# Row and column sums of the features: two of the three additions as accumulating transfers

## The chip, the cores and the metric

One core of one Trainium2 chip runs one program that computes the whole result. The metric is the device time of the program in microseconds, the median over its runs. The time before is 2430.3 us (two runs, 2430.04 and 2430.55). Engine names are those of the profile: PE is TensorE, PEld its weight loads, DVE is VectorE, ACT is ScalarE, POOL is GpSimd, SP is SyncE, whose queue issues most transfers.

## The reference

Eight sequences x of 512 tokens by 256 features go through a mixture of eight experts and a shared expert (all in float32, every expert on every token), and the gated result is added to x:

```python
g = jnp.einsum('bsd,edf->ebsf', h, Wg)
u = jnp.einsum('bsd,edf->ebsf', h, Wu)
expert_outs = jnp.einsum('ebsf,efd->ebsd', jax.nn.silu(g) * u, Wd)
expert_output = jnp.einsum('be,ebsd->bsd', gating_probs, expert_outs)
shared = jnp.einsum('bsf,fd->bsd', jax.nn.silu(h @ Sg) * (h @ Su), Sd)
sg = shared_gate_prob[:, :, None]
return (1.0 - sg) * expert_output + sg * shared      # and x is added
```

Here D = 256 and F = 1024. The gate of an expert for a sequence is one number, so the kernel multiplies the feature silu(g)*u by it ("coef") before the down product, and all experts of a sequence add up in one accumulator.

## The kernel before, in words

**Units.** The sequences are taken in two halves of four. For each half, each of the nine experts (the shared one is the ninth) and each of two groups of 512 columns of F there is a *unit*: 2 x 9 x 2 = 36 units, some 67 us each. In a unit four weight tiles i = 0..3 (128 columns of F each) meet four sequences j = 0..3, so there are sixteen features h(i, j) of 128 x 512.

**Fewer products.** The sixteen features are not made by sixteen plain products. The four diagonal ones are made in the *hub* of a unit (lines 503 to 540), and the others in *pairs*: for each (i, j) of PAIRS = (1,0), (0,2), (3,0), (1,2), (3,1), (3,2), three products give both h(j, i) and h(i, j) (R1_step and R_step, lines 549 to 571). For that, POOL makes *forms* of the weights: `at` (line 409), `u`, the difference of two `at` (w_difference, line 427), and `wb` (w_sums, line 433). The unit's `at` of tile 3 and its first `u` and `wb` are made on POOL at the start of the unit (lines 822 to 831); `at` of tiles 1 and 2 one unit ahead. The forms of the activations (`v`, `b`) are made once in the first unit, stored, and loaded again for each later unit through SP's queue, a pair or more ahead.

**Finish.** ACT takes silu of the gate product from its bank (line 490), and DVE multiplies it by the up product and by coef into a feature tile h (line 495).

**Down products.** These, too, use fewer products: for each pair two products with the pair's features and one with their difference X (line 581), and for each index n one product with the *row sum* n, the sum of h(n, l) over l, and one with the *column sum* n, the sum of h(k, n) over k. So each unit needs eight sums of four features each, three additions apiece: 24 additions of 128 x 512 on POOL (add_sum, line 589). The last unit makes its down products directly and needs no sums, so 35 units have them, 840 additions in all. The down products of a unit run from the middle of its pairs into the hub of the next unit (function `down`, line 605): first pairs 0 to 4, then row sum 0 and column sum 0, pair 5, then column sum 1, row sum 1, column sum 2, row sum 2, column sum 3 and row sum 3. Lines 634 and 657 are their matmuls.

**Order of work.** The queues of PE and POOL are written out by hand (`manual_schedule`, line 945): the main loop (lines 974 to 1011) walks a string of G (one product of gate and up) and D (one step of down), and the POOL instructions come between them. The additions are queued by h_sums after each pair (line 585 to 587), and the loop takes one from the queue at every second G of the later part of a unit (line 989) and at each of the first G of the next (line 991). Whatever is still queued when a sum is read is issued just ahead (flush_sums). The order on DVE, ACT and SP is set by the scheduler.

**Tiles.** Before, each feature has a tile of its own out of 11 (hpool), and each sum a tile out of 8 (sumpool). Six tiles of zpool hold the differences f of the hub and the rows that `prepare` loads for the second half.

Of the kernel before, what the change touches and what calls it, by code (L numbers as in the profile page):

```python
# [10 lines left out]
F32 = mybir.dt.float32  # L11
AF = mybir.ActivationFunctionType
ALU = mybir.AluOpType
# [4 lines left out]
def kernel(  # L18
# [38 lines left out]
    B, S, D = x.shape  # L57
    E, _, F = Wg.shape
    P = 128
# [15 lines left out]
    xpool = ctx.enter_context(tc.tile_pool(name="xp", bufs=4))  # L75
# [1 line left out]
    bpool = ctx.enter_context(tc.tile_pool(name="b", bufs=2))  # L77
    ppool = ctx.enter_context(tc.tile_pool(name="p", bufs=6))
    ddpool = ctx.enter_context(tc.tile_pool(name="dd", bufs=8))
    hpool = ctx.enter_context(tc.tile_pool(name="h", bufs=11))  # L80
    sumpool = ctx.enter_context(tc.tile_pool(name="sum", bufs=8))
    tpool = ctx.enter_context(tc.tile_pool(name="t", bufs=2))
    apool = ctx.enter_context(tc.tile_pool(name="ap", bufs=1))
    zpool = ctx.enter_context(tc.tile_pool(name="z", bufs=6))
    spool = ctx.enter_context(tc.tile_pool(name="s", bufs=4))
    dpool = ctx.enter_context(tc.tile_pool(name="d", bufs=2))
    iopool = ctx.enter_context(tc.tile_pool(name="io", bufs=2))
# [4 lines left out]
    ps_o = ctx.enter_context(tc.tile_pool(name="ps_o", bufs=1, space=PSUM))  # L92

    ident = const.tile([P, P], F32, name="ident")
    make_identity(nc, ident)

    gp = nc.gpsimd
# [25 lines left out]
    def issue_after(later, *first):  # L123

        for at in first:
            tc.add_manual_dep(
                later.ins,
                at.ins.name,
                mybir.DependencyInfo(
                    mybir.DependencyClass.NoSync, mybir.DependencyReason.DATA  # L130
                ),
                reason="issue order",
            )
# [25 lines left out]
    def load_rows(pool, tag, b):  # L159
        rows = []  # L160
        for c in range(2):
            if pool is not xpool:
                t = pool.tile([P, 2, D], F32, tag=tag, name=f"xin{b}_{c}")
            elif c == 0:
                both = pool.tile([P, NT, D], F32, tag=tag, name=f"xin{b}")
            if pool is xpool:
                t = both[:, 2 * c : 2 * c + 2]
            nc.sync.dma_start(
                t, x[b].rearrange("(p t) d -> p t d", t=NT)[:, 2 * c : 2 * c + 2, :]
            )  # L170
            rows.append(t)
        return rows
# [134 lines left out]
    def first_order(u, made, *what):  # L307

        if u.n == 0:
            u.issued[what] = made  # L310
            for late, early in BEHIND.items():
                if what in (late, early) and late in u.issued and early in u.issued:
                    issue_after(u.issued[late], u.issued[early])
# [67 lines left out]
    for h in range(NH):  # L381
        for e in range(NE):
            for g in range(GRP):
                u = Unit()
                u.n, u.h, u.e, u.g = len(units), h, e, g
                u.opens = e == 0 and g == 0
                u.closes = e == NE - 1 and g == GRP - 1
                u.name = f"{h}_{e}_{g}"
                u.raw, u.at, u.U, u.W, u.V, u.VB = {}, {}, {}, {}, {}, {}
                u.Ps, u.Ds, u.f, u.bank, u.h_ = {}, {}, {}, {}, {}  # L390
                u.sg, u.rows, u.cols, u.X, u.store = {}, {}, {}, {}, []
                u.sums, u.puts, u.unscaled = [], (), []
                u.ad, u.Ud, u.Wd = {}, {}, {}
                u.issued = {}
                units.append(u)

    def load_w(u, i, queue=nc.sync):
        if i not in u.raw:
            u.raw[i] = wpool.tile([P, 2, 2, P], F32, tag="w", name=f"w{u.name}_{i}")
        t = u.raw[i]  # L400
        for m in range(2):
            queue.dma_start(
                t[:, m],
                weights(u.e)[m][:, ts(NI * u.g + i, P)].rearrange(
                    "(k p) f -> p k f", p=P
                ),
            )
# [79 lines left out]
    def finish(u, m, i, j, bank):  # L487
        if m == 0:
            s = spool.tile([P, S], F32, tag="sg", name=f"sg{i}{j}_{u.name}")
            nc.scalar.activation(s, bank, AF.Silu)  # L490
            u.sg[i, j] = s
        else:
            b = NI * u.h + j
            t = hpool.tile([P, S], F32, tag="h", name=f"h{i}{j}_{u.name}")
            made = ve.scalar_tensor_tensor(  # L495
                t, u.sg[i, j], coef[:, u.e, b : b + 1], bank, ALU.mult, ALU.mult
            )
            latest_h[:] = u, made
            first_order(u, made, *(("h", i) if i == j else ("h", i, j)))
            u.h_[i, j] = t  # L500
# [27 lines left out]
    def Q_step(u, i, m):  # L528
        bank = u.bank[i, i, m]
        nc.tensor.matmul(  # L530
            bank, u.at[i][:, m], xhub[u.h, i][:, 1],
            start=False, stop=True, skip_group_check=True,
        )
        t = ddpool.tile([P, S], F32, tag="dd", name=f"D{i}{m}_{u.name}")
        u.Ds[i, m] = t
        if u.n == 0 and m == 1:
            nc.scalar.copy(t, bank)
        finish(u, m, i, i, bank)
        if u.n or m == 0:
            nc.scalar.copy(t, bank)  # L540
# [33 lines left out]
    def h_sums(u, p):  # L574


        i, j = PAIRS[p]
        if u.n + 1 == len(units):
            return
        u.X[p] = tpool.tile([P, S], F32, tag="t", name=f"X{p}_{u.name}")  # L580
        made = (gp if closes(u) and p in (1, 2, 3, 4) else ve).tensor_tensor(  # L581
            u.X[p], u.h_[j, i], u.h_[i, j], ALU.subtract
        )
        first_order(u, made, "X", p)
        for k, l in ((i, j), (j, i)):
            for which, n in (("rows", k), ("cols", l)):
                u.sums.append((which, n, (k, l)))

    def add_sum(u):
        which, n, at = u.sums.pop(0)  # L590
        sums = getattr(u, which)
        first = n not in sums
        if first:
            sums[n] = sumpool.tile([P, S], F32, tag="sum", name=f"{which}{n}_{u.name}")
        gp.tensor_tensor(sums[n], u.h_[n, n] if first else sums[n], u.h_[at], ALU.add)  # L595

    def flush_sums(u, which, n):
        while any(w == which and k == n for w, k, _ in u.sums):
            add_sum(u)

    def closes(u):

        return u.n + (2 if u.h + 1 == NH else 1) == len(units) * (u.h + 1) // NH
# [148 lines left out]
    def end_step(kind, i):  # L752

        b = NI * (NH - 1) + i
        if kind == "turn":
            t = iopool.tile([P, 2, S], F32, tag="io", name=f"end{i}")
            for r in range(2):
                ve.transpose(t[:, r], ends.pop((NH - 1, i, r)))
            ended[i] = t
        elif kind == "store":  # L760
            to = end_rows[i] = dram.tile([S, D], F32, tag=f"end{i}", name=f"endrows{i}")
            at = to.rearrange("(c r t) d -> r t c d", r=32, t=NT)
            for r in range(2):
                for q in range(4):
                    outgoing.append((
                        at[:, :, :, ts(4 * r + q, 32)],
                        ended[i][ts(q, 32), r].rearrange("r (t c d) -> r t c d", t=NT, d=32),
                    ))
        elif kind == "x":
            last_rows[i] = load_rows(xpool, "x", b)  # L770
        elif kind == "load":
            at = end_rows[i].rearrange("(p t) d -> p t d", t=NT)
            end_rows[i] = []
            for c in range(2):
                t = sumpool.tile([P, 2, D], F32, tag="sum", name=f"endin{i}_{c}")
                nc.sync.dma_start(t, at[:, 2 * c : 2 * c + 2])
                end_rows[i].append(t)
        else:
            for xr, t in zip(last_rows[i], end_rows[i]):
                gp.tensor_tensor(xr, xr, t, ALU.add)  # L780
# [31 lines left out]
    def gate_up(u, nxt):  # L812
# [12 lines left out]
        if u.n == 1:  # L825
            for _ in range(2):
                add_sum(units[0])
# [101 lines left out]
    for i in range(NI):  # L929
        c = CI[i]  # L930
# [21 lines left out]
    touch_banks()  # L952
    loaded = []
    for i in range(NI):
        loaded.append(load_rows(hpool, "h", i))
        if i:
            load_w(units[0], i)
    turning = turn_x(0, loaded)
# [8 lines left out]
    for u in units:  # L967
# [6 lines left out]
        for what in FIRST if u.n == 0 else LAST if nxt is None else OPENING if u.opens else ORDER:  # L974
            if what == "G":
# [8 lines left out]
                if nxt is None:  # L984
                    for what_, i in END_STEPS.get(nG, ()):
                        end_step(what_, i)
                if outgoing:
                    nc.sync.dma_start(*outgoing.pop(0))
                if nG > TAKE and nG % 2 == 0 and u.sums:
                    add_sum(u)  # L990
# [67 lines left out]
```

## Time and profile before

| what | value |
|---|---|
| median of the runs | 2430.3 us |
| profiled execution, first to last instruction (span) | 2427.7 us |
| PE busy | 2423.2 us (100%) |
| POOL busy | 2082.6 us (86%) |
| DVE busy | 1919.5 us (79%) |
| ACT busy | 1239.0 us (51%) |
| clock granted to PE, in every slice | 0.9 or more of full speed (mean 1.000) |
| DMA queue of SP: moved, share of 16 engines' span | 256.17 MB, 35.4% |
| POOL additions for the sums (line 595), four groups | 840, 1102.1 us |

The span is the profiled execution's own time as the profile shows it; the runs' times are taken from outside and lie 2.6 us above it. A row of the groups reads: line, engine, operation, output<-inputs by the program's names, shapes, xcount | busy us, mean ns of one | idle time of the engine just ahead of them, and what ended it. A row of a timeline reads: start in us, duration in us, engine, line and operation, and in brackets the idle time before it and who ended it. A row of waits reads: who waited <- for whom: us in total, times, the longest. In the rows of windows each engine's busy time stands with its count, then the granted clock, the DMA share and GB/s.

### The profile page before, as it was taken

To read this page: it belongs to the slowest core of one execution; us is meant where nothing else is said; L and a number is where in the kernel's file an instruction comes from. 1 tells how busy PE (TensorE), PEld (TensorE's weight loads), DVE (VectorE), ACT (ScalarE), POOL (GpSimd) and SP (SyncE) were. 2 spreads that over 40 slices of the span, in tenths; PEclk is the share of its full clock that TensorE was granted. 3 is DMA by queue.
4 is the path that set the end of the run, shared out by engine and by line. 5 is a ranking of instruction groups with operands and counts; after the bars stand their busy time and mean duration, and the time that the engine had idled before them with its cause. 6 is when DMAs were issued, how large, how long until landed. Compare 5 with 4: busy or idle time off the path is not lost.

```text
span 2427.7 us, 22771 instructions
## 1 busy us (share of the span) xinstructions
PE 2423.2 (100%) x5735; PEld 1085.3 (45%) x5735; DVE 1919.5 (79%) x2861; ACT 1239.0 (51%) x2294; POOL 2082.6 (86%) x2321
## 2 busy tenths in 40 slices
PE   9999999999999999999999999999999999999999
PEld 4444444444444444444444444444444444444446
DVE  8788888777777877787987777777877777777795
ACT  5555555554555454555455555555455555555542
POOL 7988888898988989898888888888888888888882
PEclk9999999999999999999999999999999999999999
DMA  4333333334333332334453322322333333323245
GB/s 161 108 111 107 110 98 100 117 117 126 104 122 104 103 113 94 108 112 124 119 124 110 91 84 91 92 87 90 100 104 104 95 97 90 92 87 96 79 132 145
DMA packets 221201, 257.92 MB, mean 106 GB/s; under 512 B 64016, under 2 KB 156432, under 8 KB 221072
## 3 DMA queue, kind: packets, MB, share of 16 engines
q1 hardware_dynamic: 220240, 256.17, 35.4%
q8 instruction: 48, 0.79, 0.1%
q14 instruction: 81, 0.66, 0.1%
q10 hardware_dynamic: 832, 0.30, 0.0%
HBM read 238.59 MB, written 17.83 MB: 106 GB/s over the span
## 4 chain that ended last, share of the span: by engine, by line
PE 100%; DVE 0%; issue 0%
PE c L565 31%; PE c L552 15%; PE c L530 10%; PE c L506 10%; PE r L657 7%; PE r L692 7%; PE b L634 5%; PE S L634 5%; PE q L657 5%; PE s L657 2%; PE tail L792 1%; PE B L634 0%; PE ptx L234 0%; PE touchg L372 0%; PE c L212 0%; PE ptx L208 0%
## 5 line engine op out<-in xcount | busy, mean ns | idle before, releaser
L565 PE MATMUL c<-b,wb 128*128 128x512 f32 x1728 | 847.1, 592 | 0.0
L490 ACT ACTIVATE sg<-c 128x512 f32<-128x512 f32 x576 | 343.7, 597 | 571.1 <-DVE c L570 330.3
L495 DVE SCALAR_TENSOR_TENSOR h<-sg,coef,c 128x512 f32<-128x512 f32 x576 | 427.5, 742 | 240.7 <-PE c L565 133.9
L565 PEld LDWEIGHTS c<-b,wb 128*128 128x128 f32 x1728 | 328.2, 190 | 408.8 <-issue 388.2
L552 PE MATMUL c<-v,u 128*128 128x512 f32 x864 | 441.1, 592 | 0.0
L595 POOL TENSOR_TENSOR rows<-rows,h 128x512 f32<-128x512 f32 x280 | 369.4, 1319 | 0.0
L557 DVE TENSOR_TENSOR c<-D,c 128x512 f32<-128x512 f32 x432 | 298.8, 692 | 76.7 <-ACT sg L490 57.9
L595 POOL TENSOR_TENSOR cols<-cols,h 128x512 f32<-128x512 f32 x280 | 358.8, 1281 | 0.0
L570 DVE TENSOR_TENSOR c<-c,D 128x512 f32<-128x512 f32 x432 | 298.6, 691 | 21.7 <-PE c L565 21.2
L506 PE MATMUL c<-x,w 128*128 128x512 f32 x572 | 274.5, 592 | 0.0
L442 POOL TENSOR_TENSOR wb<-u,wb 128x256 f32<-128x256 f32 x108 | 79.5, 736 | 220.1 <-ACT wb L440 220.1
L552 PEld LDWEIGHTS c<-v,u 128*128 128x128 f32 x864 | 163.6, 190 | 206.1 <-issue 164.8
L657 PE MATMUL r<-h,wd 128*128 128x512 f32 x420 | 214.5, 592 | 0.0
L692 PE MATMUL r<-X,ud 128*128 128x512 f32 x420 | 214.5, 592 | 0.0
L530 PE MATMUL c<-x,at 128*128 128x512 f32 x432 | 208.7, 592 | 0.0
L540 ACT COPY D<-c 128x512 f32<-128x512 f32 x284 | 165.6, 584 | 84.1 <-DVE h L495 84.1
L581 DVE TENSOR_TENSOR X<-h,h 128x512 f32<-128x512 f32 x202 | 199.4, 987 | 6.8
L595 POOL TENSOR_TENSOR rows<-h,h 128x512 f32<-128x512 f32 x140 | 193.4, 1382 | 0.0
L595 POOL TENSOR_TENSOR cols<-h,h 128x512 f32<-128x512 f32 x140 | 180.5, 1289 | 0.0
L512 ACT COPY P<-c 128x512 f32<-128x512 f32 x216 | 126.1, 586 | 105.5 <-PE c L506 100.9
L506 PEld LDWEIGHTS c<-x,w 128*128 128x128 f32 x572 | 108.5, 190 | 135.8 <-issue 112.4
L633 ACT COPY S<-accS 128x512 f32<-128x512 f32 x132 | 77.9, 590 | 158.4 <-DVE accV L621 140.2
(115 smaller groups left out, 3470.5 us busy)
## 6 DMA issues: line engine op xcount, KB each, us to landing
b<-xs SPq DMA_DIRECT2D x210, 512.0 KB, 3.6
v<-xs SPq DMA_DIRECT2D x210, 256.0 KB, 2.6
wd<-in_L_cond_Wd_dram SPq DMA_DIRECT2D x32, 512.0 KB, 4.8
w<-in_L_cond_Wg_dram SPq DMA_DIRECT2D x127, 128.0 KB, 3.5
w<-in_L_cond_Wu_dram SPq DMA_DIRECT2D x127, 128.0 KB, 3.6
f<-xd SPq DMA_DIRECT2D x12, 512.0 KB, 5.3
xs<-f SPq DMA_DIRECT2D x18, 256.0 KB, 2.7
xin<-in_x_dram SPq DMA_DIRECT2D x16, 256.0 KB, 3.7
```

What stands on the lines that cost most here:

```text
L490: nc.scalar.activation(s, bank, AF.Silu)
L495: made = ve.scalar_tensor_tensor(t, u.sg[i, j], coef[:, u.e, b : b + 1], bank, ALU.mult, ALU.mult)
L506: nc.tensor.matmul(bank, u.raw[i][:, m, 0], xhub[u.h, i][:, 0], start=True, stop=True)
L530: nc.tensor.matmul(bank, u.at[i][:, m], xhub[u.h, i][:, 1], start=False, stop=True, skip_group_check=True,)
L552: nc.tensor.matmul(bank, u.U[p][:, m], u.V[p], start=False, stop=True, skip_group_check=True)
L557: made = ve.tensor_sub(other, u.Ds[j, m], bank)
L565: nc.tensor.matmul(bank, u.W[p][:, r, m], u.VB[p][:, r], start=False, stop=True, skip_group_check=True,)
L570: first_order(u, ve.tensor_add(bank, bank, u.Ds[j, m]), "add", p, m)
L595: gp.tensor_tensor(sums[n], u.h_[n, n] if first else sums[n], u.h_[at], ALU.add)
L634: nc.tensor.matmul(po, w, b, start=not full, stop=True, skip_group_check=full)
L657: nc.tensor.matmul(po, w, b, start=True, stop=True)
L692: nc.tensor.matmul(A, u.Ud[p], u.X[p], start=False, stop=True, skip_group_check=True)
```

## The change

Three edits go together.

The two features of a pair, h(j, i) and h(i, j), lie side by side in one tile of 128 x 2 x 512 (`hp`, four such tiles); the diagonal features keep tiles of their own (four instead of eleven). The eight sums lie in one tile `sums` of 128 x 8 x 512 that stays for the whole program: row sum n in slot n, column sum n in slot 7 − n. The rows that the opening and the end load into sum or feature tiles go to slots of `sums` as well. zpool has five tiles instead of six.

Of the three additions of each sum, POOL makes the first, sum = h(n, n) + h, as before. The second and third are made by transfers from POOL's queue that add the source to what lies in the destination (`accum_op`). Each transfer brings a whole pair tile, 512 KB, and adds each of its two features to one sum: one transfer for pair (0,2), one for (0,3), and two each (rows, columns) for (1,2), (1,3) and (2,3). So a unit has 8 additions and 8 transfers instead of 24 additions.

The queue of a unit has 13 entries instead of 24 (an entry of four sums issues its two transfers together), so they come earlier: the loop's rule for taking one is the same.

```diff
-    hpool = ctx.enter_context(tc.tile_pool(name="h", bufs=11))
-    sumpool = ctx.enter_context(tc.tile_pool(name="sum", bufs=8))
+    hpool = ctx.enter_context(tc.tile_pool(name="h", bufs=4))
+    sumpool = ctx.enter_context(tc.tile_pool(name="sum", bufs=1))
-    zpool = ctx.enter_context(tc.tile_pool(name="z", bufs=6))
+    zpool = ctx.enter_context(tc.tile_pool(name="z", bufs=5))
+    sums = sumpool.tile([P, 8, S], F32, name="sums")
...
-            t = hpool.tile([P, S], F32, tag="h", name=f"h{i}{j}_{u.name}")
+            if i == j:
+                t = hpool.tile([P, S], F32, tag="h", name=f"h{i}{j}_{u.name}")
+            else:
+                lo, hi = min(i, j), max(i, j)
+                if (lo, hi) not in u.hp:
+                    u.hp[lo, hi] = hpool.tile([P, 2, S], F32, tag="hp", name=f"hp{lo}{hi}_{u.name}", bufs=4)
+                t = u.hp[lo, hi][:, int(i > j)]
...
+        left = []
         for k, l in ((i, j), (j, i)):
             for which, n in (("rows", k), ("cols", l)):
-                u.sums.append((which, n, (k, l)))
+                if (which, n) not in u.summed:
+                    u.summed.add((which, n))
+                    u.sums.append((((which, n),), (k, l)))
+                else:
+                    left.append((which, n))
+        if left:
+            u.sums.append((tuple(left), (min(i, j), max(i, j))))
+
+    def slot(which, n):
+        return n if which == "rows" else 7 - n
 
     def add_sum(u):
-        which, n, at = u.sums.pop(0)
-        sums = getattr(u, which)
-        first = n not in sums
-        if first:
-            sums[n] = sumpool.tile([P, S], F32, tag="sum", name=f"{which}{n}_{u.name}")
-        gp.tensor_tensor(sums[n], u.h_[n, n] if first else sums[n], u.h_[at], ALU.add)
+        if not u.sums:
+            return
+        what, at = u.sums.pop(0)
+        if len(what) == 1:
+            (which, n), = what
+            getattr(u, which)[n] = sums[:, slot(which, n)]
+            gp.tensor_tensor(sums[:, slot(which, n)], u.h_[n, n], u.h_[at], ALU.add)
+            return
+        lo, hi = at
+        pair = u.hp[at]
+        if len(what) == 4:
+            gp.dma_start(
+                sums[:, lo : hi + 1 : hi - lo], pair, accum_op=ALU.add
+            )
+            gp.dma_start(
+                sums[:, 7 - hi : 7 - lo + 1 : hi - lo], pair, accum_op=ALU.add
+            )
+        else:
+            assert {n for _, n in what} == {lo}
+            gp.dma_start(sums[:, lo : 7 - lo + 1 : 7 - 2 * lo], pair, accum_op=ALU.add)
```

**POOL at the hand-over from unit 0_3_0 to 0_3_1** (first half, expert 3, groups 0 and 1; near 460 us of the profile). In the names, `h12_0_3_0` is feature h(1, 2) of unit 0_3_0, `hp12` the tile of both features of pair (1, 2), and the last number counts tiles. Before:

```order
L421 TENSOR_TENSOR at0_3_1_2_3522<-w0_3_1_2_3519 128x256
L595 TENSOR_TENSOR cols0_0_3_0_3386<-cols0_0_3_0_3386,h30_0_3_0_3443 128x512
L595 TENSOR_TENSOR rows0_0_3_0_3406<-rows0_0_3_0_3406,h03_0_3_0_3447 128x512
L595 TENSOR_TENSOR cols3_0_3_0_3561<-h33_0_3_0_3298,h03_0_3_0_3447 128x512
L595 TENSOR_TENSOR rows1_0_3_0_3373<-rows1_0_3_0_3373,h12_0_3_0_3495 128x512
L595 TENSOR_TENSOR cols2_0_3_0_3460<-cols2_0_3_0_3460,h12_0_3_0_3495 128x512
L595 TENSOR_TENSOR rows2_0_3_0_3480<-rows2_0_3_0_3480,h21_0_3_0_3499 128x512
L430 TENSOR_TENSOR u0_3_1_0_3604<-at0_3_1_1_3465,w0_3_1_0_3412 128x256
```

And now, with the semaphores that each instruction waits for (DMASW are those of POOL's transfers, one for each of eight in turn):

```order
L424 TENSOR_TENSOR at0_3_1_2_3372<-w0_3_1_2_3369 128x256 [waits DMAHW3_49,DMAHW2_49]
L628 DMA sums_115<-hp03_0_3_0_3298 128x2x512 [waits DMASW0_49]
L620 DMA sums_115<-hp12_0_3_0_3347 128x1024 [waits DVE_49,Pool_49]
L623 DMA sums_115<-hp12_0_3_0_3347 128x1024
L620 DMA sums_115<-hp13_0_3_0_3402 128x2x512 [waits DMASW2_49,DVE_49,Pool_49]
L623 DMA sums_115<-hp13_0_3_0_3402 128x2x512 [waits DMASW3_49,Pool_49]
L620 DMA sums_115<-hp23_0_3_0_3441 128x1024 [waits DMASW4_49,DVE_49]
L623 DMA sums_115<-hp23_0_3_0_3441 128x1024 [waits DMASW5_49]
L433 TENSOR_TENSOR u0_3_1_0_3452<-at0_3_1_1_3318,w0_3_1_0_3268 128x256
```

The additions of h(3, 0) to column sum 0 and of h(0, 3) to row sum 0, and all those of pairs (1,2), (1,3) and (2,3), have become transfers; the first addition of column sum 3 stays on POOL and now stands ahead of the `at`. The additions of pairs (1,3) and (2,3) stood among the next unit's forms, and their transfers now stand ahead of its first form `u`. Each transfer of pair (1,3) waits for the landing of the transfer of pair (1,2) to the same kind of sums, and each of (2,3) for that of (1,3).

**The rest of the forms behind them**, in the change:

```order
L445 TENSOR_TENSOR wb0_3_1_0_3454<-u0_3_1_0_3452,w0_3_1_1_3315 128x256 [waits PE_49,Pool_49]
L446 TENSOR_TENSOR wb0_3_1_0_3454<-w0_3_1_0_3268,u0_3_1_0_3452 128x256
L433 TENSOR_TENSOR u0_3_1_1_3457<-w0_3_1_0_3268,at0_3_1_2_3372 128x256
L445 TENSOR_TENSOR wb0_3_1_1_3459<-u0_3_1_1_3457,w0_3_1_0_3268 128x256 [waits PE_49,Pool_49]
L446 TENSOR_TENSOR wb0_3_1_1_3459<-w0_3_1_2_3369,u0_3_1_1_3457 128x256
L426 TENSOR_TENSOR at0_3_1_3_3462<-w0_3_1_3_3413 128x256 [waits DMAHW1_49,DMAHW0_49]
L428 TENSOR_TENSOR at0_3_1_3_3462<-at0_3_1_3_3462,w0_3_1_3_3413 128x256 [waits Pool_49]
```

These seven stand in the same order as before. Line numbers of the change are larger by up to 33 (490 became 493, 495 became 504, 595 became 615, 657 became 690).

More of the change, by code (lines that the diff above doesn't have):

```diff
@@ L161, in load_rows @@
         for c in range(2):
-            if pool is not xpool:
+            if pool is sums:
+                t = sums[:, 2 * b + c].rearrange("p (t d) -> p t d", d=D)
+            elif pool is not xpool:
                 t = pool.tile([P, 2, D], F32, tag=tag, name=f"xin{b}_{c}")
@@ L391 @@
                 u.sg, u.rows, u.cols, u.X, u.store = {}, {}, {}, {}, []
-                u.sums, u.puts, u.unscaled = [], (), []
-                u.ad, u.Ud, u.Wd = {}, {}, {}
+                u.sums, u.puts, u.unscaled, u.summed = [], (), [], set()
+                u.ad, u.Ud, u.Wd, u.hp = {}, {}, {}, {}
                 u.issued = {}
@@ L584, in h_sums @@
         first_order(u, made, "X", p)
+        left = []
         for k, l in ((i, j), (j, i)):
             for which, n in (("rows", k), ("cols", l)):
-                u.sums.append((which, n, (k, l)))
-    def add_sum(u):
-        which, n, at = u.sums.pop(0)
-        sums = getattr(u, which)
-        first = n not in sums
-        if first:
-            sums[n] = sumpool.tile([P, S], F32, tag="sum", name=f"{which}{n}_{u.name}")
-        gp.tensor_tensor(sums[n], u.h_[n, n] if first else sums[n], u.h_[at], ALU.add)
+                if (which, n) not in u.summed:
[7 more added lines that the diff above has]
+        return n if which == "rows" else 7 - n
+    def add_sum(u):
+        if not u.sums:
[18 more added lines that the diff above has]
+            gp.dma_start(sums[:, lo : 7 - lo + 1 : 7 - 2 * lo], pair, accum_op=ALU.add)
     def flush_sums(u, which, n):
-        while any(w == which and k == n for w, k, _ in u.sums):
+        while any((which, n) in what for what, _ in u.sums):
             add_sum(u)
@@ L774, in end_step @@
             for c in range(2):
-                t = sumpool.tile([P, 2, D], F32, tag="sum", name=f"endin{i}_{c}")
+                t = sums[:, 2 * i + c].rearrange("p (t d) -> p t d", d=D)
                 nc.sync.dma_start(t, at[:, 2 * c : 2 * c + 2])
@@ L954 @@
     for i in range(NI):
-        loaded.append(load_rows(hpool, "h", i))
+        loaded.append(load_rows(sums, "h", i))
         if i:
```

## The prediction

> **What bounds the kernel now.** I read the page first: shares, chain, groups. Then the waits of TensorE (PE), and the timelines of one hand-over between two units.
>
> ```profile
> span 2427.7 us, 22771 instructions
> PE 2423.2 (100%) x5735; PEld 1085.3 (45%) x5735; DVE 1919.5 (79%) x2861; ACT 1239.0 (51%) x2294; POOL 2082.6 (86%) x2321
> PE 100%; DVE 0%; issue 0%
> ```
>
> The chain that ended last is PE from end to end. A busy PE may hide gaps, so I looked at what its matmuls and weight loads waited for:
>
> ```profile
> PE touchg L372 <- DVE zero L368: 1.0, 1, 1.0
> PE c L212 <- DVE x L209: 0.3, 1, 0.3
> PEld c L565 <- issue: 388.2, 1623, 0.2
> ```
>
> PE matmuls waited for other engines twice, 1.3 us in all, both in the opening. The commonest weight load shows 1,623 pauses of at most 0.2 us that waited for nothing: a steady rhythm, one matmul behind the other. So the bound is the number of matmuls, which the change leaves alone. At best the 4.5 us in which PE was not busy (2427.7 − 2423.2) could be won, 0.2%. About 2% is what a measurement of this kernel can tell from no change. The question is only whether the change makes PE wait.
>
> **What is removed.** The additions on GpSimd (POOL):
>
> ```profile
> L595 POOL TENSOR_TENSOR rows<-rows,h 128x512 f32<-128x512 f32 x280 | 369.4, 1319 | 0.0
> L595 POOL TENSOR_TENSOR cols<-cols,h 128x512 f32<-128x512 f32 x280 | 358.8, 1281 | 0.0
> L595 POOL TENSOR_TENSOR rows<-h,h 128x512 f32<-128x512 f32 x140 | 193.4, 1382 | 0.0
> L595 POOL TENSOR_TENSOR cols<-h,h 128x512 f32<-128x512 f32 x140 | 180.5, 1289 | 0.0
> DVE h L495 <- POOL rows L595: 73.4, 56, 1.9
> ```
>
> The two upper groups go: 560 additions, 728.2 us. The two lower ones, the first addition of each sum, stay. In their place stand 280 transfers of 512 KB, 8 in each of the 35 units that have sums. POOL's load of 2082.6 us falls to 1354 us plus 280 times the price of issuing one. All of this lies beside PE, as does VectorE's wait of 73.4 us for the additions, so the gain on the path is nothing. POOL stays below its present load while an issue costs less than 728/280 = 2.6 us.
>
> **What is added: a chain of waits on POOL's queue.** At the end of a unit seven transfers now stand in a row ahead of the next unit's weight forms, and the later ones wait for earlier ones to land, since they add to the same sums. How that delays the forms, I work out at the hand-over near 470 us:
>
> ```profile
> 448.67 1.20 POOL L423 TENSOR_TENSOR at<-w 128x256 f32<-128x256 f32 x1
> ...
> 454.36 0.73 POOL L442 TENSOR_TENSOR wb<-u,wb 128x256 f32<-128x256 f32 x1 [2.04 <-ACT wb L440]
> ...
> 456.96 1.19 POOL L421 TENSOR_TENSOR at<-w 128x256 f32<-128x256 f32 x1
> ...
> 465.93 0.73 POOL L430 TENSOR_TENSOR u<-at,w 128x256 f32<-128x256 f32 x1
> ...
> 469.31 0.73 POOL L442 TENSOR_TENSOR wb<-u,w 128x256 f32<-128x256 f32 x1 [0.47 <-PE c L565]
> ...
> 471.48 1.23 POOL L425 TENSOR_TENSOR at<-at,w 128x256 f32<-128x256 f32 x1
> ```
>
> ```profile
> 468.68 0.74 DVE L495 SCALAR_TENSOR_TENSOR h<-sg,coef,c 128x512 f32<-128x512 f32 x1
> ...
> 470.66 0.74 DVE L495 SCALAR_TENSOR_TENSOR h<-sg,coef,c 128x512 f32<-128x512 f32 x1
> ```
>
> ```profile
> 484.45 1.02 PE L634 MATMUL B<-cols,ad 128*128 128x512 f32 x2
> 485.30 1.02 PE L552 MATMUL c<-v,u 128*128 128x512 f32 x2
> 486.16 1.02 PE L530 MATMUL c<-x,at 128*128 128x512 f32 x2
> ```
>
> Before, POOL makes the forms from 465.93 to 472.71, 6.3 us of work without the 0.47 us wait, and the last one (at, L425) is read by the matmul at 486.16, whose weights load one half matmul (0.86/2 = 0.43 us, from 485.30 to 486.16) earlier, at 485.73: 13.0 us of cover. The start of the row does not move: the wb at 454.36 waits for ScalarE in both kernels, then come one addition and the at, and at 458.15 the transfers are next (pairs 03, then 12 twice, 13 twice, 23 twice). The second of 13 waits for the second of 12, the second of 23 for the second of 13. Three transfers (03, 12, 12) go to the DMA engines together, then one step waits for the other. With c for an issue on POOL, D for the time that one transfer takes of the DMA engines, l for its fixed latency and B for other transfers in the way:
>
> forms ready = 458.15 + (c + 3D + l) + B + (c + D + l) + c + 6.3.
>
> PE waits when that passes 485.73, so when 3c + 4D + 2l + B passes 21.3 us. The last feature (VectorE, done at 471.40) is no floor that counts: 471.40 + 2c + 6.3 stays under 485 for any c below 3.7.
>
> The trace has no accumulating transfer. The nearest rows:
>
> ```profile
> q1 hardware_dynamic: 220240, 256.17, 35.4%
> b<-xs SPq DMA_DIRECT2D x210, 512.0 KB, 3.6
> v<-xs SPq DMA_DIRECT2D x210, 256.0 KB, 2.6
> xs<-b SPq DMA_DIRECT2D x6, 512.0 KB, 2.8
> 1040.84 0.32 SPq L351 DMA_DIRECT2D b<-xs  x1
> 1048.56 0.32 SPq L351 DMA_DIRECT2D b<-xs  x1
> ```
>
> **l**: 256 KB more cost 1.0 us to landing (v against b), so 1.6 us are fixed. **D**: 35.4% of 2427.7 us for 256.17 MB is 1.76 us per 512 KB, the lower bound (one pass); two passes, 3.5 us, are the upper one, since an addition reads two tiles. The store from an on-chip tile is nearest: 2.8 − 1.6 = 1.2 us of data; both tiles read so, 2.4 us. I take **2.4**. **c**: 0.32 us as SP's issue, up to 2.54 us as the two additions that each transfer replaces (2 x 1.27, below). I take **1.2**, one addition. **B** is the DMA share of the ten microseconds after 458 and its likes at other hand-overs:
>
> ```profile
> 458.00:468.00 10.00, 10.00 (x25) 4.40 (x24) 7.37 (x12) 3.33 (x6) 9.92 (x10) 1.00 0.59 187
> 725.80:735.80 10.00, 10.00 (x24) 4.40 (x24) 7.36 (x12) 3.33 (x6) 9.92 (x10) 1.00 0.41 130
> 993.60:1003.60 10.00, 10.00 (x24) 4.40 (x24) 7.37 (x12) 3.33 (x6) 9.92 (x10) 1.00 0.56 187
> 1261.50:1271.50 10.00, 10.00 (x24) 4.37 (x23) 5.73 (x9) 5.03 (x10) 9.63 (x8) 1.00 0.87 226
> 1730.10:1740.10 10.00, 10.00 (x24) 4.37 (x23) 7.36 (x12) 3.33 (x6) 9.92 (x10) 1.00 0.29 91
> ```
>
> The last is the ordinary one (0.29, B = 2.9 us); of the 34 hand-overs after the first I take four to be fuller. With 3.6 + 9.6 + 3.2 = 16.4 us an ordinary hand-over keeps 21.3 − 16.4 − 2.9 = 2.0 us of cover: no wait. The four have B of 5.9, 4.1, 5.6 and 8.7: late by 1.0, 0, 0.7 and 3.8, together **5.5 us**.
>
> **The first hand-over** has less cover:
>
> ```profile
> 65.24 0.73 POOL L421 TENSOR_TENSOR at<-w 128x256 f32<-128x256 f32 x1
> 65.92 1.28 POOL L595 TENSOR_TENSOR cols<-cols,h 128x512 f32<-128x512 f32 x1
> 67.15 1.28 POOL L595 TENSOR_TENSOR rows<-rows,h 128x512 f32<-128x512 f32 x1
> ...
> 74.99 0.73 POOL L430 TENSOR_TENSOR u<-at,w 128x256 f32<-128x256 f32 x1
> ```
>
> ```profile
> 69.87 1.02 PE L634 MATMUL b<-rows,wd 128*128 128x512 f32 x2
> 84.46 1.02 PE L530 MATMUL c<-x,at 128*128 128x512 f32 x2
> ```
>
> Before, row sum 0 is ready at 68.43 for weights at 69.44. Now it waits for the transfer issued at 66.0, landing at 66.0 + 1.2 + 2.4 + 1.6 = 71.2: 1.8 us late. The chain behind it runs 66.0 + 16.4 + 2.9 + 4.5 (four forms of 0.73 us and the two at of unit 1) = 89.8 against 84.03: **5.8 us** late, the 1.8 included.
>
> **Edits that I cost at nothing.** The feature tiles of the pairs (four, for six pairs) now wait for transfers: pair 23 takes the tile of pair 02, whose transfer, issued at 449.9 behind the at of 448.67, lands at 455.1 by these prices, against the write at 468.68: 13 us of cover; the pairs of the next unit have more. Column sum 1, read at 484.45, is complete when the second of 13 lands, 458.15 + 2c + 4D + 2l + B = 476.3: 8 us of cover, 3 at two passes. Loads share the DMA engines: 280 x 2.4 = 672 us raise their share from 35% to 63%, and a b is loaded a pair (7.7 us, 1040.84 to 1048.56) ahead and lands in 3.6. With one z tile fewer, the last f of a hub waits for a VectorE instruction that stands ahead of it in its own queue. Behind the weight forms POOL has the forms for the down products; nine additions (11 us) fall away among them, so they come no later.
>
> **Sum.** 2427.7 + 5.8 + 5.5 = 2439.0 us of span; the median of the runs, 2430.3, lies 2.6 us above the span: **2441.6 us**.
>
> **Rivals.**
> *Two full passes* (0.20): D = 3.5 because reading the second tile is a whole transfer more. For it: the sum tile must be read back; against it: the on-chip store's 2.8 us. 3.6 + 14.0 + 3.2 + 2.9 = 23.7, late by 2.4 at each of 30 ordinary hand-overs (72), 22 at the four full ones, 10 at the first: 104.5 us, 2535 us. It decides from D = 2.9, where the ordinary cover is used up; each tenth beyond costs 35 x 0.4 = 14 us, and 2% (49 us) is passed at D = 3.1. The Trainium skill says so outright (Collectives: The Full Stack, section The bandwidth ceiling: the fold count and why AG ≠ RS ≠ AR): a reducing transfer is slower not by the adding but by its two source reads, with a measured ratio of 1.93. By that ratio on the 1.76 us, D would be 3.4 us and the time an estimated 2521 us; no run here shows it yet.
> *POOL's issue is dear* (0.09): c = 3 us or more. For it: POOL must place 128 rows or more for each; against it: nothing in the trace. 9.0 + 9.6 + 3.2 + 2.9 = 24.7, 3.4 late: 30 x 3.4 + 26 + 11 = 139 us, 2570 us. POOL's own load, 37 + 8 x 3 = 61 us of the unit's 67, would still fit.
> *Nothing waits* (0.20): D = 1.76 and c = 0.32 give 1.0 + 7.0 + 3.2 = 11.2; only the first hand-over is late, by 0.6 us: 2431 us.
> *Faster* (0.01): at most the 4.5 us, 2426.
>
> **How the numbers follow.** Forecast 0.50, 2441.6 us, alone 2433 to 2460. Forecast and "nothing waits" are within 2%: 0.70. The two dear cases make slower: 0.29. Faster: 0.01. The range runs from 2429 to 2545, which holds the two-pass case and leaves out most of the dear issue and both upper bounds together (24.8, about 6.4 late at each, near 2675).
>
> **What would show it.** Right: PE waits almost nowhere but near 70 to 90 us and at the four full hand-overs; POOL busy near 1354 us; each step of the chain from 458 on 4 to 6 us. Wrong: PE's L530 waiting for POOL's at in unit after unit (then c or D is larger), or PE's L634 and L657 waiting for a transfer, or VectorE's h waiting for one.

## The result, and the profile after

The changed kernel takes 2460.3 us (median of 2459.71 and 2460.94) against 2430.3: a ratio of 1.0124, 95% interval 1.0095 to 1.0153. That is 30 us slower and under 2%, clear of the noise. The forecast was 2441.6 us, 11 us above the kernel before. The range of 2429 to 2545 holds the time, but the band of the forecast alone, 2433 to 2460, just does not: the range reaches so far up because it takes in the rival of two full passes.

From the page of the changed kernel (span 2459.1 us in a run of 2460.94), then from its waits:

```profile
span 2459.1 us, 22864 instructions
PE 2436.0 (99%) x5735; PEld 1086.1 (44%) x5735; DVE 1923.8 (78%) x2861; ACT 1238.4 (50%) x2294; POOL 1656.0 (67%) x2041
q1 hardware_dynamic: 220240, 256.17, 34.6%
q0 software_dynamic: 58240, 146.82, 32.3%
PE 81%; DMA 9%; POOL 7%; issue 2%; DVE 1%; ACT 0%; POOLq 0%; ACTq 0%; DVEq 0%
L539 PE MATMUL c<-x,at 128*128 128x512 f32 x432 | 213.1, 603 | 14.8 <-POOL at L428 14.6
sums<-hp POOLq DMA_DIRECT2D x280, 512.0 KB, 6.6
```

```profile
PEld c L539 <- POOL at L428: 36.2, 30, 4.8
...
PE c L539 <- POOL at L428: 14.6, 16, 4.0
...
POOL sums L620 <- DMA sums<-hp: 218.1, 39, 8.3
...
POOL sums L623 <- DMA sums<-hp: 102.8, 66, 2.7
```

The chain that was PE from end to end now runs through the transfers (9%) and POOL (7%). POOL is less busy than before (67% for 86%) and yet it is what PE waits for: POOL stands still in its own queue until earlier transfers land (218 and 103 us), with the weight forms behind. Queue q0, which POOL's transfers have to themselves, took 32.3% of 2459.1 us for 280 transfers: 2.84 us of all DMA engines for each.

One hand-over on POOL's timeline, the same that the prediction worked out at 458 us, 8 us later now by the delays ahead of it, and the matmul that reads the last form:

```profile
465.05 1.19 POOL L424 TENSOR_TENSOR at<-w 128x256 f32<-128x256 f32 x1
466.18 1.20 POOL L628 DMA_DIRECT2D sums<-hp  x1
466.94 1.37 POOL L620 DMA_DIRECT2D sums<-hp  x1
467.51 1.68 POOL L623 DMA_DIRECT2D sums<-hp  x1
476.63 1.19 POOL L620 DMA_DIRECT2D sums<-hp  x1 [7.45 <-DMA sums<-hp]
479.55 1.19 POOL L623 DMA_DIRECT2D sums<-hp  x1 [1.73 <-DMA sums<-hp]
486.50 0.89 POOL L620 DMA_DIRECT2D sums<-hp  x1 [5.76 <-DVE f L530]
488.79 0.85 POOL L623 DMA_DIRECT2D sums<-hp  x1 [1.40 <-DMA sums<-hp]
489.37 1.03 POOL L433 TENSOR_TENSOR u<-at,w 128x256 f32<-128x256 f32 x1
...
494.83 0.72 POOL L428 TENSOR_TENSOR at<-at,w 128x256 f32<-128x256 f32 x1
```

```profile
495.61 1.12 PE L539 MATMUL c<-x,at 128*128 128x512 f32 x2 [1.19 <-POOL at L428]
```

From the first transfer to the first form pass 23.2 us (466.18 to 489.37); over all 35 hand-overs the mean is 21.8. The wait at 486.50 is put down to an f of VectorE, but what it needs is the sums that 13's row transfer of 476.63 adds to: a case of a wait for several semaphores. What fills the time shows in a window over the row and in the queues of the same window:

```profile
467.30:488.80 21.50, 21.50 (x52) 9.54 (x51) 16.64 (x27) 10.61 (x20) 5.16 (x7) 1.00 0.99 222
```

```profile
q0 software_dynamic: 1152, 2.82, 68.9%
q1 hardware_dynamic: 1564, 1.95, 30.0%
```

The DMA engines are 99% busy: 0.689 x 21.5 = 14.8 us for POOL's transfers, some five of them, and 0.300 x 21.5 = 6.5 us for loads.

How much each hand-over costs is read from the spacing of PE's matmuls in the trace. Back to back they start 0.43 us apart; what exceeds that (called excess spacing below) sums to 31.0 us, against 0.8 us before. The 30.2 us between them explain nearly all of the 31.4 us by which the two profiled spans differ. It falls as follows: opening 0.7 us as before, first hand-over 5.9, the four hand-overs forecast as full 1.5, 0.7, 0.8 and 7.0, two others 4.5 (near 696 us) and 1.8 (near 2390), and 8.2 in the remaining 28, of which 13 show less than 0.1 each.

### The profile page after: what moved, and what is told of

It is laid out like the page before. It is cut to its first block, busy times and chain, and to the rows that moved or that the text cites. A ratio compares the mean times of both kernels' runs of the same rounds, so it can differ in the third digit from the quotient of the medians.

```text
span 2459.1 us, 22864 instructions
## 1 busy us (share of the span) xinstructions
PE 2436.0 (99%) x5735; PEld 1086.1 (44%) x5735; DVE 1923.8 (78%) x2861; ACT 1238.4 (50%) x2294; POOL 1656.0 (67%) x2041
## 3 DMA queue, kind: packets, MB, share of 16 engines
q0 software_dynamic: 58240, 146.82, 32.3%
## 4 chain that ended last, share of the span: by engine, by line
PE 81%; DMA 9%; POOL 7%; issue 2%; DVE 1%; ACT 0%; POOLq 0%; ACTq 0%; DVEq 0%
PE c L574 27%; PE c L561 14%; DMA sums<-hp 9%; PE c L539 7%; PE c L515 6%; PE r L690 6%; PE r L725 5%; PE b L667 4%; PE S L667 4%; PE q L690 4%; PE s L690 2%; POOL wb L446 1%; POOL wb L445 1%; POOL u L433 1%; PE tail L825 1%
## 5 line engine op out<-in xcount | busy, mean ns | idle before, releaser
L504 DVE SCALAR_TENSOR_TENSOR hp<-sg,coef,c 128x512 f32<-128x512 f32 x432 | 320.7, 743 | 206.6 <-PE c L574 197.4
L620 POOL DMA_DIRECT2D sums<-hp x105 | 120.7, 1150 | 406.7 <-DMA sums<-hp 218.1
L615 POOL TENSOR_TENSOR sums<-h,hp 128x512 f32<-128x512 f32 x280 | 388.5, 1397 | 0.0
L539 PE MATMUL c<-x,at 128*128 128x512 f32 x432 | 213.1, 603 | 14.8 <-POOL at L428 14.6
L690 PE MATMUL r<-hp,wd 128*128 128x512 f32 x420 | 214.5, 592 | 0.0
L590 DVE TENSOR_TENSOR X<-hp 128x512 f32<-128x512 f32 x202 | 204.1, 1010 | 6.6
L623 POOL DMA_DIRECT2D sums<-hp x105 | 130.2, 1240 | 112.5 <-DMA sums<-hp 102.8
L667 PE MATMUL b<-sums,wd 128*128 128x512 f32 x280 | 144.7, 598 | 3.5 <-issue 3.5
```

The costliest lines, as they stand in the source:

```text
L504: made = ve.scalar_tensor_tensor(t, u.sg[i, j], coef[:, u.e, b : b + 1], bank, ALU.mult, ALU.mult)
L539: nc.tensor.matmul(bank, u.at[i][:, m], xhub[u.h, i][:, 1], start=False, stop=True, skip_group_check=True,)
L615: gp.tensor_tensor(sums[:, slot(which, n)], u.h_[n, n], u.h_[at], ALU.add)
L667: nc.tensor.matmul(po, w, b, start=not full, stop=True, skip_group_check=full)
L690: nc.tensor.matmul(po, w, b, start=True, stop=True)
```

## The experiments

Each time is compared with runs of the kernel before on the same chip, made alongside it (2430.1 us for each).

**Pair 23's transfers behind the forms.**

```diff
-                    if nG < TAKE and u.n and units[u.n - 1].sums:
+                    if 0 < nG < TAKE and u.n and units[u.n - 1].sums:
                         add_sum(units[u.n - 1])
```

> One part is moved: the two transfers of pair 23 are issued behind the next unit's first weight forms on POOL's queue, not ahead of them. In the changed kernel the forms started near 489.4 us and the at of L428 was ready at 495.9, 1.2 us late for the matmul; without the two transfers ahead of them they can start near 480, when the second transfer of 13 has been issued. Theory (the forms are late because POOL waits in order for one transfer's landing after another): the waits of L539 for POOL vanish at the ordinary hand-overs, some 23 of the 31 us go, and the first hand-over, where row sum 0 itself is late, keeps its 5 to 8 us. Median 2437 us, between 2433 and 2443. Rival (the transfers' traffic itself slows TensorE or the loads, wherever they stand in the queue): it stays within 4 us of 2460. A third outcome: column sum 2 or row sum 2 becomes late instead, seen as waits of L667 or L690 for a transfer; then 2445 or more.

Measured 2438.4 us, ratio 1.0037 (1.0023 to 1.0051). Its page:

```profile
q0 software_dynamic: 58240, 146.82, 32.7%
...
L539 PE MATMUL c<-x,at 128*128 128x512 f32 x432 | 208.8, 592 | 0.0
```

L539 waits 0.0 us, for 14.8 in the changed kernel, while each transfer takes the DMA engines as long as it did. So 22 of the 30 us were the place of two transfers in one in-order queue, not their traffic. The excess spacing left is 8.1 us: 5.4 at the first hand-over, 0.9 in the opening, and 0.2 to 0.4 at each of four matmuls that read a column sum (L690): the third outcome, in small.

**The layout alone.**

```diff
-                if (which, n) not in u.summed:
-                    u.summed.add((which, n))
+                if (which, n) not in u.summed or True:
                     u.sums.append((((which, n),), (k, l)))
+                    u.summed.add((which, n))
...
-            getattr(u, which)[n] = sums[:, slot(which, n)]
-            gp.tensor_tensor(sums[:, slot(which, n)], u.h_[n, n], u.h_[at], ALU.add)
+            first = n not in getattr(u, which)
+            getattr(u, which)[n] = to = sums[:, slot(which, n)]
+            gp.tensor_tensor(to, u.h_[n, n] if first else to, u.h_[at], ALU.add)
```

> The layout of the change is kept (pair tiles, one tile for all sums, one z tile fewer) but all 24 additions of a unit are made by POOL again, one at a time as before; no accumulating transfer is left. Theory (the layout is free, the transfers cost everything): 2430 us, between 2428 and 2433, no waits of TensorE. Rival (the shared tiles tie writers and readers together that were apart, so that VectorE's features or POOL's additions come late): 2440 us or more, with waits of VectorE's h for POOL well over the 73 us of before.

Measured 2430.5 us, ratio 1.0001 (0.9992 to 1.0010). The pair tiles, the one tile for the sums and the z tile less cost nothing, and VectorE's features wait for additions as they did (76.1 us for 73.4): all 30 us come with the transfers.

**Plain copies in place of accumulating transfers.**

```diff
-            gp.dma_start(sums[:, lo : 7 - lo + 1 : 7 - 2 * lo], pair, accum_op=ALU.add)
+            gp.dma_start(sums[:, lo : 7 - lo + 1 : 7 - 2 * lo], pair)
```

(and the same for the other two transfers.)

> The transfers stay in number, size, queue and order but only copy, so the second and third additions are left out of the sums. Theory (a transfer is long because it reads two tiles): the time on the DMA engines per 512 KB falls from 2.84 us to 1.3 to 1.8 us, a landing from 6.6 to about 4 us, the chain from the first of the seven transfers to the forms from 23 to about 14 us, and TensorE waits at the first hand-over alone: 2434 us, between 2430 and 2440. Rival (the length is that of the software queue: its issue, its descriptors, its completion): landing stays over 6 us and the time within 6 us of 2460.

Measured 2431.0 us, ratio 1.0004 (0.9995 to 1.0013). Its page:

```profile
q0 software_dynamic: 40320, 146.82, 15.9%
...
sums<-hp POOLq DMA_DIRECT2D x280, 512.0 KB, 3.7
```

A transfer that only copies takes 0.159 x 2429.3 / 280 = 1.38 us of the DMA engines, the adding one 2.84: 2.06 times as much. The row of seven, first transfer to first form, falls from 21.8 to 14.9 us. Even the first hand-over is on time. That is the theory's outcome, with 3 us less than it left for the first hand-over. The Trainium skill (Collectives: The Full Stack, section The bandwidth ceiling: the fold count and why AG ≠ RS ≠ AR) says that a reducing transfer is slower by its two source reads, with a ratio of 1.93, measured there on collectives between ranks. The trace agrees in the ratio, with 2.06; it shows the time and not the reads. The adding transfers also come in more packets (58240 against 40320), but the number is not the reason: a packet of the same 4096 bytes takes 0.328 us when it adds and 0.159 when it copies (medians over the two traces).

**One weight form made twice.**

```diff
         t = atpool.tile([P, 2, P], F32, tag="at", name=f"at{u.name}_{i}")
+        if CI[i] == 2.0:
+            gp.tensor_tensor(t, raw[:, :, 0], raw[:, :, 1], ALU.add)
         at_of(t, CI[i], raw[:, :, 0], raw[:, :, 1])
```

> POOL makes the first addition of the weight form at of index 3 twice in every unit, 1.2 us more, behind the transfers and ahead of the forms that TensorE waits for. Theory (POOL's chain at the hand-over sets the end, with no cover left at nearly all of the 34 hand-overs): 1.2 us more at each, about 35 to 45 us in all, 2500 us, between 2490 and 2515. Rival (the lost time comes from something beside POOL's chain, and the waits for POOL are only where it shows): less than 6 us more, at most 2466.

Measured 2485.6 us, ratio 1.0231 (1.0215 to 1.0246): 25 us above the changed kernel, between the two expectations and outside both bands. POOL's timeline shows the size that was wrong (two lines more in the code, so L428 and L430 here are L426 and L428 above):

```profile
500.32 0.73 POOL L419 TENSOR_TENSOR at<-w 128x256 f32<-128x256 f32 x1
501.13 0.73 POOL L428 TENSOR_TENSOR at<-w 128x256 f32<-128x256 f32 x1
501.93 0.73 POOL L430 TENSOR_TENSOR at<-at,w 128x256 f32<-128x256 f32 x1
```

The extra addition costs 0.81 us of the queue (500.32 to 501.13), not 1.2. 35 x 0.81 = 28 us; the excess spacing grew from 31.0 to 58.6, by 27.6 (the profiled run took 2488.7 us, 28 above that of the changed kernel). Now 32 of the 35 hand-overs cost 0.1 us or more, where 22 did. So nearly the whole addition arrives at PE: hardly any cover was left, and of the 13 hand-overs that had cost less, ten now cost 0.77 us or more.

**The first unit's sums by additions**, alone and together with the forms first. The edit is that of the layout run, with `u.n == 0` in place of `True`.

> One part is undone, in one unit of 36: the sums of the first unit are made by POOL's additions; all other units keep the transfers and their order. Theory: the two waits of the first hand-over (3.6 us at 69 us of the span and 0.8 us at 89, with the half clock behind the first stall 2.1 us more) go, nothing else changes: 2454 us, between 2451 and 2457. Rival (TensorE's time at the first hand-over comes back later, because the following hand-overs have no cover and every one pays what the one before did not): 2458 or more.

> Two parts: pair 23's transfers stand behind the next unit's first forms, as in the run that moved them alone (2438.4 us), and the sums of the first unit are made by POOL's additions throughout, so that row sum 0 of that unit waits for no transfer. Theory (what was left there is the first hand-over alone: the matmul with row sum 0 at 69.2 us waited 3.6 us and the next ones ran at half the clock for another 2.1): 2432 us, between 2430.5 and 2433.5; the small waits of 0.2 to 0.4 us of L690 for column sum 2 may stay. Rival (some cost of the transfers is spread over the program, and forms that come early only hide a part of it): 2435 us or more.

Measured 2455.5 us alone, ratio 1.0108 (1.0093 to 1.0124), and 2433.0 us for both, 1.0013 (1.0004 to 1.0022). Alone, 4.8 us are saved by the medians. The four runs lie between 2452.9 and 2459.6 us, so the time by itself does not exclude the rival; the traces do: the first hand-over costs nothing, and the other 34 together show an excess spacing of 24.2 us, for 24.4 in the changed kernel. Both together leave 2.9 us; the excess spacing is 3.1 us, 1.2 of it in the opening and 1.6 at three places where L691 (L690 above) reads a column sum late. A cost spread over the program, the rival, does not show. It does not beat the kernel before, and the bound of PE leaves little to beat it by.

**One transfer of the seven left out.**

```diff
             assert {n for _, n in what} == {lo}
+            if hi == 3:
+                return
             gp.dma_start(sums[:, lo : 7 - lo + 1 : 7 - 2 * lo], pair, accum_op=ALU.add)
```

> One transfer of eight in each unit is left out, that of pair 03, so that row sum 0 and column sum 0 lack their third addition. It is the first of the seven in a row; no later transfer waits for it, since 12, 13 and 23 add to other sums. Theory (the row is long because the DMA engines are full: it lasts as long as five transfers of 2.84 us and some 5 us of loads take of them): the row is 2.8 us shorter, nearly all ordinary waits of L539 go, and so does that for row sum 0 at the first hand-over; a few us stay at the hand-overs near 696 and 1306 us: 2434 us, between 2431 and 2440. Rival (the row is a chain of fixed latencies, 12 before 13 before 23, whatever else the engines do): only the first hand-over gains, 2452 us or more.

Measured 2436.4 us, ratio 1.0025 (1.0016 to 1.0035): as the theory had it, and far below the rival's 2452. The same hand-over on its POOL timeline, first issue and last, and the first form:

```profile
460.93 0.91 POOL L620 DMA_DIRECT2D sums<-hp  x1
...
478.90 0.85 POOL L623 DMA_DIRECT2D sums<-hp  x1 [2.75 <-DMA sums<-hp]
479.47 1.03 POOL L433 TENSOR_TENSOR u<-at,w 128x256 f32<-128x256 f32 x1
```

From the first L620 to the first form it is 18.5 us here and was 22.4; over all 35 the means are 18.4 and 21.0. The row is 2.7 us shorter for a transfer that no other waits for, about the 2.84 us that it took of the DMA engines. So the row is bound by the engines' time and not by a chain of fixed latencies.

**Stalls made on purpose**, in the kernel before, one run each, for something seen in the trace after (below): the at of tile 3 is begun n more times over in eight units.

```diff
+        for _ in range(STALL.get(u.n, 0) if i == 3 else 0):
+            gp.tensor_tensor(t, raw[:, :, 0], raw[:, :, 1], ALU.add)
         at_of(t, CI[i], raw[:, :, 0], raw[:, :, 1])
```

> The kernel before, with TensorE made to wait on purpose in eight of its 36 units: POOL makes the first addition of the at of index 3 another 19, 20, 21, 22, 23, 24, 26 and 30 times over in units 4, 7, 10, 13, 22, 25, 28 and 31, 0.7 us each, against the 13 us of cover that the hand-over has. TensorE should stand still for about 1, 2, 3, 3, 4, 5, 6 and 9 us there. Theory (a granted clock of a half follows a stall that is long by itself, over some 3 us, and lasts 3.4 us or twice that): the matmuls behind the longer stalls come 0.85 us apart for 3 to 7 us, those behind stalls of under 3 us never. Rival (the half clock comes from the accumulating transfers or their load on the memory): no matmul in this kernel comes 0.85 us apart, whatever the stall, since it has no such transfer.

> The kernel with stalls made on purpose again, with fewer additions: 5, 6, 7, 8, 9, 10, 12 and 14 in place of 19 to 30. By the slope of the run before (12.1 us of stall at 19 additions, 0.8 us for each more) the stalls should be near 0.9, 1.7, 2.5, 3.3, 4.1, 4.9, 6.5 and 8.1 us, 2465 us in all. Theory (the half clock is a matter of the stall's length, and sets in at some 3 us): matmuls 0.85 us apart behind the last five, never behind the first three. Rival (any pause of a microsecond or two can bring it, depending on where it falls): half clock behind some of the first three, or none behind some of 4 us and more.

Measured 2569.6 and 2480.5 us. In the first all eight stalls were far longer than worked out, 11.5 to 20 us, because what came late was not the form but the column sums behind it, which had less cover; all eight brought the half clock, in a kernel without a single accumulating transfer, so the rival falls. PE in the second, at a stall of 2.69 us and at one of 3.48:

```profile
900.45 1.13 PE L659 MATMUL q<-cols,ad 128*128 128x512 f32 x2 [2.69 <-POOL cols L597]
901.41 1.02 PE L554 MATMUL c<-v,u 128*128 128x512 f32 x2
...
907.77 1.13 PE L636 MATMUL B<-cols,ad 128*128 128x512 f32 x2 [1.91 <-POOL cols L597]
908.74 1.60 PE L554 MATMUL c<-v,u 128*128 128x512 f32 x2
910.13 1.91 PE L567 MATMUL c<-b,wb 128*128 128x512 f32 x2
```

```profile
1510.62 2.08 PE L659 MATMUL q<-cols,ad 128*128 128x512 f32 x2 [3.48 <-POOL cols L597]
1512.48 1.92 PE L554 MATMUL c<-v,u 128*128 128x512 f32 x2
```

Two matmuls in a row take 1.02 us at the full clock and 1.9 at half. The three units whose stalls were at most 1.9 us showed no half clock; the stalls of 3.48, 4.28, 5.87 and 7.49 us all did. Between them length does not decide: behind 2.69 us the matmuls of 901 ran full, and the half clock came from 909 on, behind a second stall of only 1.91, while four other stalls of 1.9 us brought none. So the theory holds for long stalls and fails below: for the short ones the rival is right that it depends on where the stall falls. The last section shows where. The time is some 15 us above the 2465 worked out: in three units a second column sum was late, so that the pauses sum to 35 us where 32 were expected, and the half clock behind them cost some 12 us more.

## Why the prediction was right, and where its sum was short

**The bound, and the place.** Right. PE was full, nothing could be won, and what was lost lies where forms are late behind a row of transfers. The forecast's mechanism is shown by the run that moves pair 23 and by the form made twice. The layout cost nothing, as said. But the loss is 30 us where 11 were forecast, and the prediction's own signs say so: POOL's at was late in hand-over after hand-over (L539, L530 before), which it had named as the sign that c or D is larger, and L667 (L634 before) waited once for a row sum (below). At the hand-over shown, the steps from 13's transfers to 23's were 9.9 and 9.2 us (476.63 to 486.50, 479.55 to 488.79), not 4 to 6.

**c, 1.2 us.** The issues show 1.15 (L620) and 1.24 us (L623):

```profile
L620 POOL DMA_DIRECT2D sums<-hp x105 | 120.7, 1150 | 406.7 <-DMA sums<-hp 218.1 <-DVE accV L656 101.2 <-DVE f L530 24.9
L623 POOL DMA_DIRECT2D sums<-hp x105 | 130.2, 1240 | 112.5 <-DMA sums<-hp 102.8 <-issue 7.7 <-DMA w<-in_L_cond_Wu_dram 2.0
```

As taken, though the next instruction starts 0.6 to 0.8 us after (466.18, 466.94, 467.51). POOL's load was forecast at 1354 + 280 x 1.2 = 1690 us and is 1656; the 1354 us among the prediction's signs left the issues out. The rival of a dear issue falls.

**D, 2.4 us: the step that failed.** It is 2.84. To take one pass twice was right (2.06 times); the pass was too short. The prediction had it as 1.2 us, the landing of a store less a fixed part that was read from loads; the copy between two on-chip tiles takes 1.38. The threshold that the rival of two full passes named, 2.9, is nearly met, and so the hand-overs stand at the edge: 22 of 35 cost 0.1 us or more, where four were forecast late. This rival's mechanism, a second full pass, was right and its price of 3.5 too high, since the loads' 1.76 us was not the unit to double.

**4D + 2l and B: wrong in their make-up, and by luck nearly right in their sum.** For the last issue two transfers of 12, one of 03 and both of 13 must be through, five and not four; with copies, at 1.46 us less for each, the row fell by 6.9 us, 4.7 transfers' worth. And B was read over ten microseconds, while the row lasts over twenty. The trace of before had the numbers for that:

```profile
458.00:481.00 23.00, 23.00 (x55) 10.10 (x54) 18.25 (x29) 10.90 (x20) 22.13 (x27) 1.00 0.33 104
1730.10:1753.00 22.90, 22.90 (x54) 10.07 (x53) 18.14 (x29) 10.86 (x20) 22.03 (x27) 1.00 0.20 63
```

0.33 x 23 = 7.6 us where 5.9 was taken, and 0.20 x 22.9 = 4.6 at an ordinary hand-over where 2.9 was. Against these the formula added three issues and two latencies, 6.8 us, which mostly lie beneath the engines' time. 5 x 2.84 + 4.6 = 18.8; the mean row of 21.8 leaves 3.0 us, which are taken to be starting and landing and were not measured by themselves. With the same 3.0 the sum gives 14.5 us for the copies (14.9 measured) and 19.0 without pair 03 (18.4). The forecast for an ordinary hand-over was 19.3 with 2.0 us of cover; the mean of 21.8 uses that up and 0.5 more. So of the 2.5 us that were missing, D makes 1.8, the fifth transfer 2.8 and B 1.7, and the issues and latencies take 3.8 back.

**The four full hand-overs**, forecast late by 1.0, 0, 0.7 and 3.8 us, cost 1.5, 0.7, 0.8 and 7.0. The two of 4.5 and 1.8 us were not forecast. Of the 7.0 and of the 4.5, some 2.7 and 1.6 us are the half clock of the last section, for which the forecast had no term.

**The first hand-over**, 5.8 us forecast, 5.9 measured; that the two agree is luck, since the parts do not. On POOL's timeline and on PE's:

```profile
66.56 1.18 POOL L628 DMA_DIRECT2D sums<-hp  x1
67.32 1.33 POOL L620 DMA_DIRECT2D sums<-hp  x1
67.89 1.64 POOL L623 DMA_DIRECT2D sums<-hp  x1
```

```profile
68.80 1.88 PE L539 MATMUL c<-x,w 128*128 128x512 f32 x4
74.17 1.19 PE L667 MATMUL b<-sums,wd 128*128 128x512 f32 x2 [3.49 <-issue]
75.15 3.52 PE L515 MATMUL c<-x,w 128*128 128x512 f32 x4
```

Row sum 0 was 3.5 us late and not 1.8, since the transfers of 12, issued 0.8 and 1.3 us behind its own, shared the DMA engines with it, and a load did too; then the four matmuls at 75.15 took 3.52 us, 1.88 being their time at full clock. The forms behind, which were to add the other 4.0, added 0.4 us.

**What was costed at nothing** stayed at nothing: no wait of VectorE's features for a transfer, and no load too late (b lands in 4.3 us for 3.6, 7.7 ahead; the two of the row at 467 us took 8.9, and nothing waited for them).

## What to carry to other kernels

Work that is taken off a busy engine and given to transfers is not free when the same in-order queue issues them and must wait for one before the next: cost the queue's standing still, not its busy time. Add up what the DMA engines must move in the stretch that the row itself lasts, loads included, and count an accumulating transfer between on-chip tiles as two plain ones (2.84 against 1.38 us for 512 KB here). Where waits cannot be taken out, put what others wait for ahead of them; here that one line gave back 22 of 30 us.

## What the runs showed of the hardware beyond that

A stall of TensorE can cost more than itself. Behind three stalls of the changed kernel, of 3.49 us (near 71), 2.67 (near 698) and 4.01 (near 1308), the granted clock fell to a half. The window behind the second shows it:

```profile
699.70:703.10 3.40, 3.14 (x4) 1.51 (x5) 0.00 (x0) 1.03 (x2) 3.24 (x8) 0.50 0.00 0
```

The clock stays there for 3.4 us, or 6.8 behind the stall of 4.0 us, and the matmuls run 0.85 us apart for 0.43. About 6 of the 31 us are this (half of the 3.4, 3.1 and 5.5 us in which matmuls ran at half speed). The Trainium skill (TensorE: Matmul & The Clock Gate, section HAM oscillation — how this bites in real kernels) has it as a rule to leave no idle gap over about 3.4 us. The runs agree from 3.42 us up; below, a stall of 2.67 us had it too, and in the run with a form made twice one stall of 3.33 us had it and one had not (two matmuls take 2.02 us behind the first and 1.12 behind the second):

```profile
91.68 2.02 PE L541 MATMUL c<-x,at 128*128 128x512 f32 x2 [3.33 <-POOL at L430]
...
707.86 1.12 PE L541 MATMUL c<-x,at 128*128 128x512 f32 x2 [3.33 <-POOL at L430]
```

So length does not decide. What does shows in the traces: in every run the half clock begins and ends on one grid of stretches of 3.413 us (in the changed kernel it lasts from 75.0 to 78.4, 699.7 to 703.1 and 1310.7 to 1317.5 us; its beginnings are 183 and 179 stretches apart), and what counts is how long PE pauses within one stretch. By the grid of the run with a form made twice, the first stall lies in one stretch, with 0.12 us of PE's work left in it, and the second in two, with 1.7 in each:

```profile
88.40:91.80 3.40, 0.12 (x1) 0.12 (x2) 1.42 (x3) 0.00 (x0) 3.17 (x6) 1.00 0.31 60
702.80:706.20 3.40, 1.72 (x5) 0.42 (x3) 3.40 (x7) 0.00 (x0) 3.32 (x5) 1.00 0.63 125
706.20:709.60 3.40, 1.74 (x4) 0.87 (x5) 0.67 (x2) 0.58 (x2) 3.17 (x7) 1.00 0.02 5
```

In the run of the short stalls it is the same: the 2.69 us fell across a border (at 898.9), the 1.91 us behind it into one stretch (905.7 to 909.1). Over all eleven traces, each of the 20 stretches at full clock with 2.2 us of pause or more was followed by the half clock, and none of those with 1.7 or less; of two between, the one with 1.91 was and one with 2.00 was not. The clock came back behind a stretch in which PE paused for at most 0.35 us. This was read from the runs afterwards; none was made to test it. Where the grid falls differs from run to run, so a stall of some 2 to 3.4 us can bring the half clock in one run and not in another.
